# A selective-scan kernel: the gate's second half goes to GpSimd, a row copy goes to VectorE between two halves of a store, and a product is left whole

## The chip, the cores and the metric

The kernel runs on one core of a Trainium2 chip. Its time is device microseconds of that core, as the median of several executions. Tensor work goes to TensorE (PE), and the rest is shared by VectorE (DVE), ScalarE (ACT) and GpSimd (POOL). SyncE (SP) issues most DMAs, GpSimd's queue the others.

## What is computed

Two layers follow each other on an image batch of shape (8, 128, 128, 128). Layer 0 is linear attention with a layer norm and a residual. Layer 1 is a two-dimensional selective scan. The change is in the second part of layer 1, which in the reference reads (cut):

```python
delta = softplus(dt_weight @ dt + bias);  du = delta * u
x_t = exp(delta_t * A) * x_(t-1) + du_t * B_t          # the scan along L, four directions
y   = sum over the four directions of C_t * x_t + D * u
yz  = y * silu(z)                                      # the gate
mu  = yz.mean(-1);  var = ((yz - mu)**2).mean(-1)
out = (gamma * (yz - mu) / sqrt(var + 1e-5) + beta) @ Wout
```

## The kernel before

`layer0` and `layer1_front` write the scan's inputs to DRAM: `ubs` (u times B, in two orders), `xps` (the small rows for delta and C), `zs` (the finished silu(z)) and `gs` (a summand of y). `layer1_scan` reads them. It goes through 8 outer rounds `o`, each of 4 scan slots of 16 chunks, so 512 steps; a chunk is 1024 positions for two halves `c` of 128 channels. All four slots of a round add into one SBUF accumulator `y`.

A step `n` works as follows (line numbers are those of the profile of before):

- `delta` (L973, PE) multiplies into a PSUM tile `px`; `soften` (L977, ACT) makes `sp` by softplus; `decay` (L981, ACT) turns `px` into the factor exp(A times delta); `weigh` (L994, L996, POOL) makes `h`, the product of `ubt` and `sp`; `scan` (L1004, L1006, DVE) runs the recurrence on `px` and `h`, once for each c.
- `spread` (L1012, PE) spreads the C rows over partitions and `emit` (L1024 and others, DVE) multiplies them onto `h`, in two halves; `gather` (L1046, DVE) and `add` (L1054, POOL) add to `y` in the slots after the first.

In the 16 steps after a round's four slots, the chunks of that finished round leave. These are the steps called leaving; they coincide with the first slot of the next round, and after the last round they run without scans. For a leaving chunk, in order: `fetch` loads two tiles `z` (L1070, SP), `gate` multiplies `y` onto `z`, one call for each half (L1074), `square` (L1077, ACT) writes the squares over `y`, `moments` (L1087, PE) makes the rows `pm` of means, `keep` copies `pm` from PSUM to SBUF as `sr` (L1093), `to_tokens` (L1099, PE) turns it into `pq`, `square_mean` (L1103, ACT) makes `mv`, `variance` (L1107, L1108, DVE) makes the variance, `deviation` (L1112, L1113, ACT) its inverse root `rstd`, `project` (L1120, PE) multiplies `z` by the output weights into a `px` tile, and `store` (L1126, DVE, four instructions for each half; L1130 the DMA) scales and writes out. The second half of this chain is one step later than the first: `store` and `deviation` of a chunk run in the step after its `project`.

Every engine's instructions are issued in the order written in `step`. `px` has three buffers, `h` two, `z` six and `r` two. `project` writes into the `px` tile that `scan(n, 1)` has finished with, and that tile is held until the next step's `store` has read it; the second `delta` of the next chunk is written there. In ten or so steps around each leaving group GpSimd's queue also issues `add_d` (L946), an accumulating DMA of 1 MB onto `y`.

Of the kernel before, what the change touches and what calls it, by code (L numbers as in the profile page):

```python
# [11 lines left out]
ALU = mybir.AluOpType  # L12
# [19 lines left out]
CW = CH // H  # L32
# [756 lines left out]
def layer1_scan(ctx: ExitStack, tc, ubs, xps, zs, gs, dtw, dtb, a_log, gamma, beta, w_out, out):  # L789
# [15 lines left out]
    nc = tc.nc  # L805
# [36 lines left out]
    for i in range(3):  # L842
        t = const.tile([P, CH], BF16, name=f"rows{i}")
# [3 lines left out]
    for i in range(3):  # L847
        t = const.tile([P, D2], BF16, name=f"dtw{i}")
# [92 lines left out]
    ubt, sp, da, hs, leaving = {}, {}, {}, {}, {}  # L941
# [6 lines left out]
    def load_rows(n):  # L948
        sl, i = units[n]
        m = sl.at(i)  # L950
        rw = rws[n % 3]
        md = NCH - 1 - m if sl.dt_turned_back else m
        src = xps[sl.dt_image, sl.dt_order].rearrange("j r l -> (j r) l")
        for j in range(3):
            nc.sync.dma_start(rw[3 * NR * j : 3 * NR * j + 3 * NR, :], src[:, md * CH : md * CH + CH])
        nc.sync.dma_start(rw[96:99, :], xps[sl.b, sl.order, :, R + 1, m * CH : m * CH + CH])

    def load(n, c):
        sl, i = units[n]
        m = sl.at(i)  # L960
        ubt[n, c] = wp.tile([P, CH], F32, name="ubt", tag="ub", bufs=4)
        nc.sync.dma_start(ubt[n, c], ubs[sl.b, sl.order, c][:, m * CH : m * CH + CH])
# [16 lines left out]
    def decay(n, c):  # L979
        sl, i = units[n]  # L980
        nc.scalar.activation(da[n, c], sp[n, c], AF.Exp, scale=sa[:, sl.s, c : c + 1])  # L981

    def weigh(n, c):
        if c == 0:
            hs[n] = wp.tile([P, NC2, CH], F32, name="h", bufs=2)
        u, t, h = ubt.pop((n, c)), sp.pop((n, c)), hs[n][:, c, :]
        if units[n][0].permuted:
            u = u.rearrange("p (e h w) -> p h e w", e=2, w=W // 2)
            t, h = (v.rearrange("p (h e w) -> p h e w", e=2, w=W // 2) for v in (t, h))
        else:  # L990
            u, t, h = (v.rearrange("p (h w) -> p h w", w=W) for v in (u, t, h))
        if n in leaving and c == 0:
            for s in (slice(0, CW // 2), slice(CW // 2, CW)):
                nc.gpsimd.tensor_tensor(h[:, s], u[:, s], t[:, s], ALU.mult)  # L994
        else:
            nc.gpsimd.tensor_tensor(h, u, t, ALU.mult)  # L996

    def scan(n, c):
        sl, i = units[n]
# [14 lines left out]
    def emit(n, hf):  # L1014

        sl, i = units[n]
        h = hs[n][:, :, hf * 512 : hf * 512 + 512]
        c = cps.pop((n, hf)).to_broadcast([P, NC2, GN])  # L1020
        if sl.place == 0:
            v = sl.y_at(i, hf)
            split = "p c (a b) -> p c a b"
            nc.vector.tensor_tensor(v, h.rearrange(split, b=H), c.rearrange(split, b=H), ALU.mult)  # L1024
            return
        if hf != sl.first:
            nc.vector.tensor_tensor(h, h, c, ALU.mult)  # L1027
            return
        p = da.pop((n, 1))
        if sl.y_turned:  # L1030
            ts[n] = p.rearrange("p (c b a) -> p c b a", c=NC2, a=GW)
            t = p.rearrange("p (c b a) -> p c a b", c=NC2, a=GW)
            split = "p c (a b) -> p c a b"
            nc.vector.tensor_tensor(t, h.rearrange(split, b=H), c.rearrange(split, b=H), ALU.mult)
        else:
            t = p.rearrange("p (c q) -> p c q", c=NC2)
            ts[n] = t.rearrange("p c (a b) -> p c a b", b=H)
            nc.vector.tensor_tensor(t, h, c, ALU.mult)  # L1038

    def gather(n):  # L1040

        sl, i = units[n]
        v = sl.y_at(i, sl.first)
        if sl.y_turned:
            v = v.rearrange("p c a b -> p c b a")
        nc.vector.tensor_tensor(v, v, ts.pop(n), ALU.add)  # L1046
# [12 lines left out]
    def piece(m, hf):  # L1059
        return y[:, :, (2 * m + hf) * GN : (2 * m + hf + 1) * GN]  # L1060

    def mirrored(o, m, hf):
        p = 2 * m + hf
        return 2 * NCH - 1 - p if o % 2 == 1 else p

    def fetch(o, m):
        for hf in range(2):
            zt[m, hf] = z = wp.tile([P, NC2, GN], F32, name="z", bufs=6)
            p = mirrored(o, m, hf)
            nc.sync.dma_start(z, zs[o].rearrange("c p l -> p c l")[:, :, p * GN : p * GN + GN])  # L1070

    def gate(o, m, hf, eng):
        z, ym = zt[m, hf], piece(m, hf)
        eng.tensor_tensor(z, ym[:, :, ::-1] if o % 2 == 1 else ym, z, ALU.mult)  # L1074

    def square(m, hf):
        nc.scalar.activation(piece(m, hf), zt[m, hf], AF.Square)  # L1077
# [12 lines left out]
    def keep(m):  # L1090
        pm = pts[m, "rows"]
        pts[m, "rows"] = sr = wp.tile([P, GN], F32, name="sr", bufs=1)
        nc.scalar.copy(sr, pm)  # L1093

    def to_tokens(m):
        sr = pts.pop((m, "rows"))
# [13 lines left out]
    def deviation(m):  # L1110
        rstd = rst[m]
        nc.scalar.activation(rstd, rstd, AF.Ln)  # L1112
        nc.scalar.activation(rstd, rstd, AF.Exp, scale=-0.5)  # L1113
# [8 lines left out]
    def store(o, m, hf):  # L1122
        po, rstd = pts.pop((m, hf)), rst[m]
        r = wp.tile([P, GW, P], F32, name="r", bufs=2)
        for w in range(GW):
            nc.vector.scalar_tensor_tensor(r[:, w, :], po[:, w, :], rstd[:, w, hf : hf + 1], bw, ALU.mult, ALU.add)  # L1126
        s = slice(mirrored(o, m, hf) * GW, mirrored(o, m, hf) * GW + GW)

        dst = out[o].rearrange("a e c -> e a c") if o % 4 < 2 else out[o]
        nc.sync.dma_start(dst[:, s, :], r)  # L1130
# [6 lines left out]
    for o in range(B):  # L1137
        n = (o + 1) * K * NCH
# [14 lines left out]
    def step(n):  # L1153
        live = 0 <= n < N
        then = n + 1 < N
        before = 1 <= n <= N
        now, last, soon, later = (leaving.get(n + i) for i in (0, -1, 1, 2))
        first = before and units[n - 1][0].place == 0
        if before:
            half1 = units[n - 1][0].first  # L1160
            emit(n - 1, half1)
            if not first:
                gather(n - 1)
        if now and last:
            gate(*now, 1, nc.vector)
        if before:
            emit(n - 1, 1 - half1)
        if n + 2 < N:
            load_rows(n + 2)
        if n in fetched:  # L1170
            fetch(*fetched[n])
        if last:
            nc.scalar.preload_act_table_set("natural_log_exp_and_others")
        if live:
            decay(n, 0)
        if now:
            square(now[1], 1)
        if live:
            decay(n, 1)
        if last:  # L1180
            deviation(last[1])
        if live:
            weigh(n, 0)
            if n + 2 < N:
                load(n + 2, 0)
        if live:
            weigh(n, 1)
            if n + 2 < N:
                load(n + 2, 1)
        if now:  # L1190
            moments(now[1])
        if live:
            scan(n, 0)
            da.pop((n, 0))
        if last:
            for hf in range(2):
                store(*last, hf)
        if then:
            for c in range(NC2):
                delta(n + 1, c)  # L1200
        if now:
            keep(now[1])
        if then:
            soften(n + 1, 0)
        if now:
            to_tokens(now[1])
            square_mean(now[1])
        if then:
            soften(n + 1, 1)
        if live:  # L1210
            scan(n, 1)
        if first:
            hs.pop(n - 1)
        if now:
            variance(now[1])
        if live:
            half1 = units[n][0].first
            spread(n, half1, "pc")
            spread(n, 1 - half1, "pt")
        if soon and now:  # L1220
            gate(*soon, 0, nc.gpsimd)
        elif soon:
            gate(*soon, 1, nc.gpsimd)
        elif later:
            gate(*later, 0, nc.gpsimd)
        if soon:
            square(soon[1], 0)
        if now:
            p = da.pop((n, 1)) if live else px.tile([P, CH], F32, name="px")
            for hf in range(2):  # L1230
                project(now[1], hf, p[:, hf * 512 : hf * 512 + 512])
        elif live and units[n][0].place == 0:
            da.pop((n, 1))
        if before and not first:
            add(n - 1)
            hs.pop(n - 1)
        if n in weighed:
            units[weighed[n]][0].weights()
        if n in summed:
            add_d(*summed[n])  # L1240
# [78 lines left out]
```

## Time and profile before

| | us |
|---|---|
| Three runs | 9049.44, 9056.5, 9060.8 (median 9056.5) |
| The profiled execution's own time | 9056.52 |
| Its span, first to last instruction | 9054.7 |

| Engine | busy us (share of the span) |
|---|---|
| PE | 6274.4 (69%) |
| DVE | 8055.0 (89%) |
| ACT | 7094.7 (78%) |
| POOL | 7222.8 (80%) |

The mean granted TensorE clock is 0.799. The scans begin near 4350 us and end near 8915 us. A step outside the leaving groups takes 8.22 us. The eight leaving groups begin near 4863, 5445, 6023, 6605, 7183, 7766, 8347 and 8915 us; the seven with scans last 176 to 182 us each, the last one without scans 140 us. Times inside the span are counted from its start. In a line of the timeline, the first two numbers are the start and the length; in brackets is the idle time of the engine before it and what ended that.

### The profile page before, as it was taken

How to read it: one execution, taken by the hardware profiler on the slowest of the kernel's cores; microseconds unless marked ns; L12 is line 12 of the kernel's file. 1: busy time of each engine (PE TensorE's matmuls, PEld its weight loads, DVE VectorE, ACT ScalarE, POOL GpSimd, SP SyncE). 2: the span in 40 equal slices, each digit the busy share in tenths (PEclk: the TensorE clock that was granted, in tenths of full speed). 3: DMA queues.
4: the chain of work that ended last, by engine and by line, in shares of the span. 5: the costliest groups of instructions: out<-in, count | busy, mean ns of one | idle time of the engine just before them, and what ended most of it. 6: DMA issues, size and time to landing. Idle time of an engine off the chain costs nothing. (4 is left out here: it accounts for less than half of the span.)

```text
span 9054.7 us, 91854 instructions
## 1 busy us (share of the span) xinstructions
PE 6274.4 (69%) x24350; PEld 3062.4 (34%) x24512; DVE 8055.0 (89%) x8337; ACT 7094.7 (78%) x8318; POOL 7222.8 (80%) x4676
## 2 busy tenths in 40 slices
PE   8999999998999999997335437355363453644636
PEld 5656655564333333332003204022040230411303
DVE  6777777777999999998899999999999999999996
ACT  5666666665999999997787888878888888888886
POOL 3656765646789888888698897988979989899796
PEclk9999999999999999999556658566585575755857
DMA  1332323423687888888559678596785876958767
GB/s 78 136 119 112 129 101 149 163 91 140 216 245 251 250 244 244 243 245 251 168 170 254 179 211 243 166 244 192 200 255 154 243 205 188 260 155 226 227 177 211
DMA packets 934775, 1750.71 MB, mean 193 GB/s; under 512 B 150228, under 2 KB 376148, under 8 KB 926064
## 3 DMA queue, kind: packets, MB, share of 16 engines
q1 hardware_dynamic: 873328, 1509.92, 50.6%
q0 software_dynamic: 60928, 234.90, 14.1%
q8 instruction: 200, 3.28, 0.1%
q14 instruction: 319, 2.61, 0.1%
HBM read 1052.36 MB, written 692.12 MB: 193 GB/s over the span
## 5 line engine op out<-in xcount | busy, mean ns | idle before, releaser
L973 PE MATMUL px<-rows,dtw 128*128 128x512 bf16 x1893 | 913.5, 575 | 2291.7 <-DVE y L1046 1079.4
L996 POOL TENSOR_TENSOR h<-ubt,sp 128x1024 f32<-128x1024 f32 x912 | 2173.0, 2413 | 244.6 <-DMA rows<-xps 82.7
L575 DVE SCALAR_TENSOR_TENSOR acc<-xb,cw,acc 128x1024 f32<-128x1024 f32 x1024 | 1320.3, 1289 | 132.9 <-ACT xb L543 89.9
L567 POOL TENSOR_TENSOR tap<-tap 128x1024 f32<-128x1024 f32 x512 | 1223.2, 2392 | 249.1 <-ACT tap L565 225.3
L977 ACT ACTIVATE sp<-px 128x1024 f32<-128x1024 f32 x1024 | 1045.9, 1024 | 434.2 <-PE px L973 383.9
L973 PEld LDWEIGHTS <-dtw 128*128 128x128 bf16 x2048 | 166.0, 110 | 3084.3 <-issue 1016.0
L1006 DVE TENSOR_TENSOR_SCAN h<-px,h 128x1024 f32<-128x1024 f32 x512 | 1178.1, 2332 | 34.4 <-POOL h L996 19.0
L1004 DVE TENSOR_TENSOR_SCAN h<-px,h 128x1024 f32<-128x1024 f32 x512 | 1178.8, 2332 | 24.7 <-POOL h L994 9.5
L1054 POOL TENSOR_TENSOR y<-y,h 128x512 f32<-128x512 f32 x768 | 1162.9, 1561 | 4.0 <-DVE h L1027 4.0
L981 ACT ACTIVATE px<-sp,sa 128x1024 f32<-128x1024 f32 x1024 | 1110.2, 1109 | 6.1
L556 PE MATMUL acc<-xi,wt 128*128 128x512 f32 x2048 | 937.6, 600 | 55.0 <-ACT ures L580 55.0
L565 ACT ACTIVATE tap<-xb,cw 128x1024 f32<-128x1024 f32 x768 | 837.3, 1139 | 14.6 <-POOL xb L540 14.5
L977 ACT ACT_TABLE_LOAD x512 | 656.9, 1283 | 159.3 <-PE px L973 125.5
L994 POOL TENSOR_TENSOR h<-ubt,sp 128x512 f32<-128x512 f32 x224 | 368.0, 1692 | 281.6 <-ACT mv L1103 202.2
L1120 PEld LDWEIGHTS px<-wg,z 128*128 128x128 f32 x4096 | 551.1, 217 | 113.0 <-issue 107.9
L1012 PE MATMUL pc<-rows,csel 128*128 128x512 bf16 x1017 | 514.2, 587 | 83.0 <-DVE rstd L1107 73.9
L556 PEld LDWEIGHTS acc<-xi,wt 128*128 128x128 f32 x2048 | 374.8, 189 | 575.1 <-issue 412.5
L1120 PE MATMUL px<-wg,z 128*128 128x128 f32 x4096 | 551.3, 300 | 0.0
L286 POOL TENSOR_TENSOR q<-q,qs 128x512 f32<-128x512 f32 x256 | 270.3, 1056 | 314.1 <-DVE qs L285 250.0
L981 ACT ACT_TABLE_LOAD x400 | 513.2, 1283 | 7.1
L529 PE MATMUL pxb<-xi,wi 128*128 128x512 f32 x1024 | 496.4, 607 | 3.4 <-ACT xb L538 2.0
L1046 DVE TENSOR_TENSOR y<-y,px 128x1024 f32<-128x1024 f32 x384 | 468.6, 1220 | 14.4
(156 smaller groups left out, 15263.1 us busy)
## 6 DMA issues: line engine op xcount, KB each, us to landing
ubt<-ubs SPq DMA_DIRECT2D x1024, 512.0 KB
zs<-z SPq DMA_DIRECT2D x512, 256.0 KB
ubs<-ures SPq DMA_DIRECT2D x256, 512.0 KB
ubs<-turned SPq DMA_DIRECT2D x256, 512.0 KB
z<-zs SPq DMA_DIRECT2D x256, 512.0 KB
y<-gs POOLq DMA_DIRECT2D x128, 1024.0 KB, 10.1
gs<-du POOLq DMA_DIRECT2D x96, 1024.0 KB, 8.6
rows<-xps SPq DMA_DIRECT2D x1536, 60.0 KB
```

What stands on the lines that cost most here:

```text
L556: nc.tensor.matmul(acc[:, s, :], wt[:, j, c, :], x, start=(j == 0), stop=(j == len(ON_PE) - 1))
L565: nc.scalar.activation(t, at(n, c, *d), AF.Copy, scale=weight(n, c, *d))
L567: nc.gpsimd.tensor_tensor(sums[n, c], sums[n, c], t, ALU.add)
L575: nc.vector.scalar_tensor_tensor(acc, at(n, c, *d), weight(n, c, *d), acc, ALU.mult, ALU.add)
L973: nc.tensor.matmul(p[:, hf * 512 : hf * 512 + 512], sl.dw[:, c * P : c * P + P], src, start=True, stop=True)
L977: nc.scalar.activation(t, da[n, c], AF.Softplus)
L981: nc.scalar.activation(da[n, c], sp[n, c], AF.Exp, scale=sa[:, sl.s, c : c + 1])
L996: nc.gpsimd.tensor_tensor(h, u, t, ALU.mult)
L1004: nc.vector.tensor_tensor_scan(e[:, ::-1], x[:, ::-1], e[:, ::-1], start, ALU.mult, ALU.add)
L1006: nc.vector.tensor_tensor_scan(e, x, e, start, ALU.mult, ALU.add)
L1054: nc.gpsimd.tensor_tensor(v[:, c], v[:, c], h[:, c], ALU.add)
L1120: nc.tensor.matmul(po[:, w, :], z[:, c, w * H : w * H + H], wg[:, c, :], start=(c == 0), stop=(c == NC2 - 1))
```

## The change

Three edits, all in the leaving steps. First, both halves of the gate are made by GpSimd, at the end of the step before the one that uses them; before, GpSimd made the first half there, and VectorE made the second at the beginning of the using step, between the two `emit`s. Second, `keep` becomes a VectorE copy, and its place is between the two halves of `store`; before, it was a ScalarE copy ahead of `soften`. Third, GpSimd's product in `weigh` for c = 0, which the leaving steps made in two halves of 128x512, is one instruction of 128x1024.

```diff
@@ weigh
-        if n in leaving and c == 0:
-            for s in (slice(0, CW // 2), slice(CW // 2, CW)):
-                nc.gpsimd.tensor_tensor(h[:, s], u[:, s], t[:, s], ALU.mult)
-        else:
-            nc.gpsimd.tensor_tensor(h, u, t, ALU.mult)
+        nc.gpsimd.tensor_tensor(h, u, t, ALU.mult)
@@ keep
-        nc.scalar.copy(sr, pm)
+        nc.vector.tensor_copy(sr, pm)
@@ step
-        if now and last:
-            gate(*now, 1, nc.vector)
@@ step
         if last:
-            for hf in range(2):
-                store(*last, hf)
+            store(*last, 0)
+        if now:
+            keep(now[1])
+        if last:
+            store(*last, 1)
         if then:
             for c in range(NC2):
                 delta(n + 1, c)
-        if now:
-            keep(now[1])
@@ step
         if soon and now:
-            gate(*soon, 0, nc.gpsimd)
+            for hf in range(2):
+                gate(*soon, hf, nc.gpsimd)
         elif soon:
             gate(*soon, 1, nc.gpsimd)
```

## The prediction

> **What bounds the kernel now.** The page's first part comes first. It says that VectorE is the fullest engine, but as an average over stages.
>
> ```profile
> PE 6274.4 (69%) x24350; PEld 3062.4 (34%) x24512; DVE 8055.0 (89%) x8337; ACT 7094.7 (78%) x8318; POOL 7222.8 (80%) x4676
> ```
>
> The change touches only the leaving steps, so I went to the table of stretches for one group (the one that begins at 6023 us): its steps 1 to 7, and then 8 to 14.
>
> ```profile
> 6033.45:6121.05 87.60, 66.56 (x420) 48.22 (x426) 75.39 (x105) 66.66 (x84) 62.72 (x33) 0.84 0.92 273
> 6121.05:6194.70 73.65, 60.19 (x437) 41.74 (x443) 72.18 (x106) 67.10 (x85) 56.21 (x29) 0.98 0.83 254
> ```
>
> The columns are length, busy PE, PEld, DVE, ACT, POOL, granted clock, DMA share, GB/s. In steps 8 to 14 VectorE is busy 72.2 of 73.65 us: 10.5 us a step, nothing free. Steps 1 to 7 are 14 us longer with a DMA share of 0.92; the list of waits says why (`store` waits for its output buffer):
>
> ```profile
> PE px L973 <- DVE r L1126: 186.0, 110, 6.0
> DVE r L1126 <- DMA out<-r: 65.4, 26, 6.0
> POOL z L1074 <- DMA z<-zs: 44.6, 10, 9.1
> ```
>
> A full VectorE suggests that VectorE sets the step. The timeline of one steady step (12th of the group) asks for more care:
>
> ```profile
> 6173.73 2.35 DVE L1004 TENSOR_TENSOR_SCAN h<-px,h 128x1024 f32<-128x1024 f32 x1
> ...
> 6176.02 2.16 DVE L1126 SCALAR_TENSOR_TENSOR r<-px,rstd,bw 128x128 f32<-128x128 f32 x8
> ...
> 6176.60 0.58 ACT L1093 COPY sr<-pm 128x512 f32<-128x512 f32 x1 [0.61 <-PE pm L1087]
> ...
> 6178.23 0.59 PE L973 MATMUL px<-rows,dtw 128*128 128x512 bf16 x2 [1.34 <-DVE r L1126]
> ...
> 6178.66 0.95 PE L1099 MATMUL pq<-sel,sr 128*128 128x4 f32 x8
> ...
> 6179.65 0.18 ACT L1103 ACTIVATE mv<-pq 128x8 f32<-128x8 f32 x1
> 6179.72 1.02 ACT L977 ACTIVATE sp<-px 128x1024 f32<-128x1024 f32 x1
> ...
> 6180.63 1.06 ACT L1077 ACTIVATE y<-z 128x1024 f32<-128x1024 f32 x1
> ...
> 6181.70 1.28 ACT L1173 ACT_TABLE_LOAD   x1
> ...
> 6183.00 1.12 ACT L981 ACTIVATE px<-sp,sa 128x1024 f32<-128x1024 f32 x1
> ...
> 6184.22 2.35 DVE L1004 TENSOR_TENSOR_SCAN h<-px,h 128x1024 f32<-128x1024 f32 x1
> ```
>
> Read it as one chain with no gap: scan 0 starts at 6173.73, the store ends at 6178.18, and only then may the second `delta` be written (its tile held the projection that the store reads); `pq` stands behind that `delta` on PE, `mv` behind `pq`, the second softplus behind `mv`, then a square, the table load, the decay, which ends at 6184.12, and the next scan 0. That is 10.49 us, and every link starts within 0.1 us of the one before. VectorE's own instructions, start to start, make 10.35 us. So two rings are nearly tied, and the one through PE and ScalarE is ahead by 0.14. The last step of the group decides between them: it has neither the gate nor the square.
>
> ```profile
> 6201.58 2.34 DVE L1024 TENSOR_TENSOR y<-h,pc 128x1024 f32<-128x1024 f32 x2
> 6204.25 2.29 DVE L1004 TENSOR_TENSOR_SCAN h<-px,h 128x1024 f32<-128x1024 f32 x1 [0.33 <-ACT px L981]
> ```
>
> Without the gate (1.22 us) VectorE stands idle for 0.33 us waiting for the decay; the step is 9.54 us, shorter by 0.95. That is the square's place on ScalarE (from the second softplus to the table load it is 1.98 us above, and 1.03 in step 15), not the gate's on VectorE.
>
> **Edit 1, the gate.** 120 VectorE gates of 1.22 us (146 us) go; GpSimd gains 120 of 2.36 us (its own gates' median; 283 us). On VectorE that shortens the ring that is second, so it gives nothing by itself. On GpSimd a steady step now has 2.33 + 2.34 (weigh) + 2 x 2.35 (gates), 9.4 us, against the 8.2 of before. Its first product must wait for scan 1 of the step before (6180.44 in the step above; it starts at 6180.57), because `h` has two buffers. GpSimd was idle 2.3 us there. With the ring found below (11.09) it would be idle for 11.09 - 9.4 - 0.13 = 1.6 us, so the cover holds; with `add_d` (1.2 us) behind the gates it still holds, by 0.4. It doesn't hold in step 0, where `add` is queued behind the gates and the next products behind `add`. There GpSimd has no gap (6024.15 gate, 6026.47 add, 6029.92 product to 6033.42, scan at 6033.45): a second gate adds 2.3, the undivided product takes off 1.1, so +1.2 us once a group. The earlier gate also needs its `z` earlier; where GpSimd already waits for the first `z` (10 times, none in a steady step) the second follows it.
>
> **Edit 2, the copy.** ScalarE loses 128 copies of 0.585 us (75 us). They stand ahead of the table load and the first softplus; the softplus was done at 6179.52 and `mv` started at 6179.65, behind `pq`. ScalarE had time there, so nothing comes back. VectorE gains 128 copies of 128x512 out of PSUM. The trace has no such copy; two rows bound it: 0.29 us (128x128 out of PSUM, L879) and 0.68 us (128x512 with one PSUM operand, L300). I take 0.68, because 129 columns out of PSUM (L253, 0.283) cost what one column a cycle and a fixed part cost. Consecutive instructions overlap by 0.08 (eight of 0.342 in 2.16 us), so 0.60 in the queue.
>
> Behind the copy stand the second half of the store, scan 1, the variance and the emits. Waiting for the store are the second `delta`, `pq`, `mv`, the second softplus, the square, the table, the decay and scan 0: the leading ring. Before, the copy was beside it. Now the ring is 10.49 + 0.60 = 11.09 us. `pm` is ready at 6176.57; the copy's turn would come at 6173.73 + 2.29 + 1.04 = 6177.06, so it doesn't usually wait; where the clock is low `pm` is up to 1.2 us later, and then the store waits too.
>
> The page "VectorE: DVE Perf Modes" of the Trainium skill (section "The perf-mode tier table") allows a copy out of PSUM up to twice the rate. By its cycle table that is (120 + 256) / 0.96, an estimate of 0.39 us, 0.31 in the queue, and the sum below would be 28 us instead of 49. No run here shows a double rate out of PSUM.
>
> **Edit 3, the product.** 112 products of 1.28 + 2.28 us (the second stretched by 1.0 beside VectorE's gate) become 2.38. GpSimd's saving of 1.1 us a step shortens the wait ahead of scan 0, which is now not the last to arrive: nothing, except in step 0, counted above.
>
> **The sum.** A group with scans:
> - step 0: +1.2;
> - steps 1 to 7: 7 x 0.60 = +4.2. They take 86.5, 83.0, 87.6, 82.8, 88.6, 84.4 and 84.3 us in the seven groups against 73.4 for seven steady ones, so 12 us a group are DMA backlog. A slower pace lets the backlog shrink. If the transfers set the time, the 5.4 of steps 0 to 7 are hidden; if not, none. The share of 0.92 is near full: I count a third, 1.8;
> - steps 8 to 15: 8 x 0.60 = +4.8.
>
> That makes 6.6 a group, 46 for seven. The last group has no scans; there PE's chain moments, copy, `pq`, project (7.3 us a step) holds the copy, 0.68 for 0.585: 16 x 0.1 = 1.6, and perhaps as much for `z` waited for earlier: 3. In all +49. The profiled execution (9056.52, span 9054.7) is the median of the runs, so 9106.
>
> Ends: everything hidden in steps 0 to 7, 34 + 2, is 9092; nothing hidden, 7 x 10.2 + 3, is 9131; with a late `pm` in some steps up to 9150; with the short copy (0.29, 0.21 in the queue) and all hidden, about 9070.
>
> **Rivals.**
> - *VectorE is the ring.* Then 1.13 goes and 0.60 comes, -0.53 in 105 steps, -56, with step 0's +8: 9008. It decides if the decay isn't what scan 0 waits for. For it: 72.2 busy of 73.65. Against it: the idle 0.33 in step 15. Chance 0.09.
> - *All is hidden*: the transfers set more steps than I think, or the copy is short. 9056 to 9074. Chance 0.08.
> - *The port.* L1108, 8 columns, takes 0.17 us in most steps and up to 2.38 where a GpSimd instruction runs; it is issued at 6180.53, 0.04 ahead of GpSimd's product. If it now falls behind an undivided product, it waits 2.4 and the emits with it: the step becomes 6.71 + 0.60 + 2.5 + 2.5 = 12.3, 1.8 more than now in 105 steps, 9245. Both start from scan 1's end as before, so the order should stand. Chance 0.05.
>
> The page "SBUF — State Buffer" (section "Who interferes with whom") gives the rule: the port that VectorE shares with GpSimd is locked for a whole instruction. L1108's rows agree, and by the rule leaving the product whole doubles the longest block.
>
> **How the numbers follow.** The forecast has 0.78, up to 9150. A measurement of this kernel tells 0.2%, 18 us, from no change. Faster 0.09, same 0.08, slower 0.83. The range 9064 to 9150 leaves out the first rival, the third, and the edges of the others.
>
> **What would show it.** Right: steady steps near 11.1 us, scan 0 idle before on ScalarE's L981 by about 0.9, the copy at 0.68 directly ahead of the second four stores, step 0 near 11.8, GpSimd idle some 1.6 a step. Wrong: steady steps at 10 us (first rival), L1108 over 2 us in steady steps (third), or a copy near 0.4.

## The result, and the profile after

The changed kernel takes **9131.1 us** (median of 5 runs, 9119.2 to 9137.9) against 9056.5 (9049.4 to 9060.8): a ratio of 1.0079, 95% interval [1.0065, 1.0093], slower by 74.6 us. Its profiled execution took 9129.67 (span 9127.9), 73.15 more than the one of before, and all sums below are made against that difference.

The page's first part:

```profile
PE 6321.5 (69%) x24512; PEld 3073.3 (34%) x24512; DVE 8042.8 (88%) x8345; ACT 7023.1 (77%) x8190; POOL 7378.0 (81%) x4684
```

VectorE's and ScalarE's shares fell, GpSimd's rose, and the span grew by 73 us. The table of stretches for the group that now begins at 6041.69 (step 0, steps 1 to 7, steps 8 to 14; columns as before):

```profile
6041.69:6053.50 11.81, 7.98 (x57) 5.28 (x50) 11.60 (x7) 8.96 (x11) 11.73 (x7) 0.93 0.84 230
6053.50:6137.65 84.15, 66.06 (x433) 46.55 (x434) 70.61 (x105) 61.26 (x74) 71.07 (x33) 0.86 0.93 277
6137.65:6216.30 78.65, 63.03 (x437) 43.96 (x435) 68.72 (x106) 63.49 (x78) 65.35 (x29) 0.93 0.78 238
```

Steps 8 to 14: 78.65 us where they took 73.65, with VectorE *less* busy (68.7 for 72.2). In step 0 GpSimd has no gap. One steady step in the timeline (the 11th of that group), from scan 0 to scan 0:

```profile
6171.40 2.35 DVE L1000 TENSOR_TENSOR_SCAN h<-px,h 128x1024 f32<-128x1024 f32 x1 [1.26 <-ACT px L981]
...
6173.69 1.13 DVE L1122 SCALAR_TENSOR_TENSOR r<-px,rstd,bw 128x128 f32<-128x128 f32 x4
...
6174.74 0.68 DVE L1089 COPY sr<-pm 128x512 f32<-128x512 f32 x1
...
6175.34 1.11 DVE L1122 SCALAR_TENSOR_TENSOR r<-px,rstd,bw 128x128 f32<-128x128 f32 x4
...
6176.50 0.59 PE L973 MATMUL px<-rows,dtw 128*128 128x512 bf16 x2 [1.72 <-DVE r L1122]
...
6177.92 0.18 ACT L1099 ACTIVATE mv<-pq 128x8 f32<-128x8 f32 x1 [0.74 <-PE pq L1095]
...
6182.49 2.35 DVE L1000 TENSOR_TENSOR_SCAN h<-px,h 128x1024 f32<-128x1024 f32 x1 [1.27 <-ACT px L981]
```

The step is 11.09 us. The copy stands between the store's halves, the second `delta` (L973) waits for the second half, `mv` for the `pq` behind it, and scan 0 waits 1.27 us for the decay.

By stretches, summed over the seven groups with scans (after less before):

| stretch | measured | forecast |
|---|---|---|
| step 0 | +8.3 | } 12.6 for steps 0 to 7 |
| steps 1 to 7 | +10.6 | } |
| steps 8 to 14 | +34.9 | 29.4 |
| step 15 | +2.3 | 4.2 |
| last group, without scans | +14.2 | 3 |
| before the first scan, untouched | +4.0 | 0 |
| other steps, untouched | -1.2 | 0 |
| all | +73.15 | +49 |

### The profile page after: what moved, and what is told of

Same layout as the page of the kernel before. It is cut to its first block, busy times and chain, and to the rows that moved or that the text cites. A ratio compares the mean times of both kernels' runs of the same rounds, so it can differ in the third digit from the quotient of the medians.

```text
span 9127.9 us, 92102 instructions
## 1 busy us (share of the span) xinstructions
PE 6321.5 (69%) x24512; PEld 3073.3 (34%) x24512; DVE 8042.8 (88%) x8345; ACT 7023.1 (77%) x8190; POOL 7378.0 (81%) x4684
## 5 line engine op out<-in xcount | busy, mean ns | idle before, releaser
L992 POOL TENSOR_TENSOR h<-ubt,sp 128x1024 f32<-128x1024 f32 x1024 | 2410.0, 2393 | 458.6 <-ACT mv L1099 161.8
L973 PE MATMUL px<-rows,dtw 128*128 128x512 bf16 x2048 | 954.9, 565 | 2280.5 <-DVE y L1042 1058.6
L973 PEld LDWEIGHTS <-dtw 128*128 128x128 bf16 x2048 | 165.5, 110 | 3111.1 <-issue 1045.3
L1070 POOL TENSOR_TENSOR z<-y,z 128x1024 f32<-128x1024 f32 x256 | 615.2, 2472 | 48.0 <-DMA z<-zs 45.8
```

Source lines behind the costliest of these rows:

```text
L973: nc.tensor.matmul(p[:, hf * 512 : hf * 512 + 512], sl.dw[:, c * P : c * P + P], src, start=True, stop=True)
```

## The experiments

Each ratio compares with runs of the kernel before that were taken along with the experiment (medians 9050.9 to 9058.2 us). Steps and stretches are read from one profiled execution of each kernel and compared with the profile of before; single executions of one kernel lie up to 33 us apart, so a few us in one stretch mean little.

Two new things in the trace of after had to be placed. The copy comes late in some steps (15 of 49 steady steps are over 11.4 us), and one small VectorE instruction, the variance's `tensor_scalar` (L1104, 128x8, 0.17 us alone), can take far longer. All its executions, and one in the timeline beside GpSimd:

```profile
L1104 DVE TENSOR_SCALAR rstd<-rstd x128: 170/171/11657, 4872.4 to 9118.9; 128x8 f32<-128x8 f32 x128
```

```profile
5472.26 5.12 POOL L992 TENSOR_TENSOR h<-ubt,sp 128x1024 f32<-128x1024 f32 x2
...
5472.64 9.61 DVE L1104 TENSOR_SCALAR rstd<-rstd 128x8 f32<-128x8 f32 x1
5476.91 5.08 POOL L1070 TENSOR_TENSOR z<-y,z 128x1024 f32<-128x1024 f32 x2
```

Durations are least/median/most in ns. In step 1 of five groups it stays open through four GpSimd instructions that follow each other without a gap; in the last group's first step it takes 11.66 us. In three of the five groups the two emits and the next scan, which read one operand from PSUM, start meanwhile, and they are open until the same moment as the small instruction, 0.25 us after the last of the four; whether they too wait for GpSimd isn't shown:

```profile
6646.07 1.19 POOL L946 DMA_DIRECT2D y<-gs  x1
...
6646.56 10.27 DVE L1104 TENSOR_SCALAR rstd<-rstd 128x8 f32<-128x8 f32 x1
...
6646.64 10.20 DVE L1020 TENSOR_TENSOR y<-h,pc 128x1024 f32<-128x1024 f32 x2
...
6650.25 6.58 DVE L1002 TENSOR_TENSOR_SCAN h<-px,h 128x1024 f32<-128x1024 f32 x1
```

"Excess" below is the time of all 128 beyond 0.17 each: 39 us before (most: 2.38), 100 after.

### Each half of the change alone

**copy_only**: the kernel before with edit 2.

```
-        nc.scalar.copy(sr, pm)
+        nc.vector.tensor_copy(sr, pm)
...
-            for hf in range(2):
-                store(*last, hf)
+            store(*last, 0)
+        if now:
+            keep(now[1])
+        if last:
+            store(*last, 1)
```

> The kernel before with edit 2 alone: the copy on VectorE between the halves of the store; VectorE keeps its gate and the product stays divided. If scan 0 is set by the ring store, second delta, pq, mv, second softplus, square, table, decay (A), a steady leaving step is 10.49 + 0.60 = 11.09 us with scan 0 waiting about 0.1 us for the decay, as in the changed kernel, step 0 stays at 10.62, and no variance instruction waits more than 2.4 us. With half of the 4.2 us of steps 1 to 7 hidden by the transfers and 4.8 in steps 8 to 15, 7 x 6.9 + 2 = +50: 9106 us. If VectorE's queue sets it (B), a steady step is 10.35 + 0.60 = 10.95 with no wait for the decay, some 9090 us.

Measured 9108.3, ratio 1.0064 [1.0051, 1.0076]. The steady step is 11.08, step 0 10.62 as before, steps 8 to 14 +34.6, the last group +10.0, steps 1 to 7 only +3.7; the excess is 19 us.

**gate_only**: edits 1 and 3; the copy stays on ScalarE, at its old place.

```
-        if now and last:
-            gate(*now, 1, nc.vector)
...
-            gate(*soon, 0, nc.gpsimd)
+            for hf in range(2):
+                gate(*soon, hf, nc.gpsimd)
```

> The changed kernel without edit 2: the copy is on ScalarE again, at its old place; both gates on GpSimd, product whole. A: VectorE is relieved of 1.13 us a step but a steady step stays at 10.49 us, with scan 0 waiting about 1 us for the decay; step 0 is 11.8 (GpSimd), and the variance instruction of step 1 and of the last group's first step is caught behind GpSimd for 8 to 12 us as in the changed kernel, part of it hidden by the transfers: +8 for step 0, +14 in the last group, 0 to 20 in steps 1 to 7: 9078 to 9098 us. B: steady steps under 10 us and a time under 9010.

Measured 9070.3, ratio 1.0020 [1.0011, 1.0029]. A steady step:

```profile
6161.74 2.35 DVE L1000 TENSOR_TENSOR_SCAN h<-px,h 128x1024 f32<-128x1024 f32 x1 [1.26 <-ACT px L981]
...
6172.23 2.35 DVE L1000 TENSOR_TENSOR_SCAN h<-px,h 128x1024 f32<-128x1024 f32 x1 [1.26 <-ACT px L981]
```

It is 10.49 us, as before: VectorE lost its gate and spends the time waiting for the decay. Step 0 is 11.81 (+8.3 in all), and the excess is 128 us, so the long waits come with edits 1 and 3. They cost next to nothing here: summed over the seven groups, steps 1 and 2 are 35 us longer than before, but steps 3 to 7, where the kernel before has its backlog of transfers, are 35 us shorter, and the last group is only 2.5 longer. The halves, +57.4 and +19.4 by their own comparisons, make 76.8 against 74.6 for the whole.

### What the small instruction's wait costs

**var_psum**: the changed kernel, with the variance's difference left in PSUM, so that L1104's successor (L1105) reads PSUM.

```
+        v = pts.pop(m)[:, :, :, 1]
+        nc.vector.tensor_tensor(v, v, mv.pop(m), ALU.subtract)
+        nc.vector.tensor_scalar(rstd, v, 0.0, EPS1, ALU.max, ALU.add)
```

> The changed kernel with the variance's difference left in PSUM, so that the second of its two small VectorE instructions reads PSUM and writes SBUF instead of SBUF to SBUF. If that instruction's long waits (3.7 to 4.2 us in step 0, 9.6 to 10.3 in step 1 of five groups, 11.7 in the last group) are for the port that VectorE shares with GpSimd, they are gone and it takes under 0.3 us everywhere; the last group loses about 10 us, steps 1 to 7 a few us a group at most because the transfers hide a part: 9095 to 9121 us. If it waits for something else, a result of GpSimd for one, the long waits stay, and the time is that of the changed kernel within 8 us. Steady steps stay at 11.08 or rise by the second spread, which now waits for one more small instruction.

Measured 9150.7, ratio 1.0110 [1.0096, 1.0123]. No execution is long any more:

```profile
L1105 DVE TENSOR_SCALAR rstd<-pq x128: 166/167/168, 4868.3 to 9127.3; 128x8 f32<-128x8 f32 x128
```

But the time was missed by 30 us, to the wrong side. Steps 8 to 14 are +48.4, many at 11.7 to 12.9, and steps 1 to 7 are +12.2 although no execution waits. The second `spread` writes the PSUM bank that `pq` sits in and now waits for one instruction more (TensorE idle 0.92 us ahead of it, for 0.70); the projections and `pm` follow it. That this is the whole cause isn't shown.

**first_gate**: the changed kernel, with the second gate of each group's second chunk on VectorE again.

```
+        if now and last and n - 2 not in leaving:
+            gate(*now, 1, nc.vector)
...
-            for hf in range(2):
+            for hf in range(2 if last else 1):
```

> The changed kernel, but the second gate of a group's second chunk is made by VectorE between the emits as before; all other gates stay on GpSimd. If step 0 costs +1.2 because of that gate in GpSimd's queue, step 0 is back at 10.6 or below (the product is whole, so down to 10.0). If the variance instruction's long waits need a GpSimd queue that never pauses, they shrink to under 4.5 us in step 1 and in the last group, because GpSimd has its gap again. Then -8 to -12 for step 0, some -10 in the last group and a few in steps 1 to 7: 9095 to 9112 us. If the accumulating DMAs of GpSimd's queue cause the waits, they stay at 9 to 12 us.

Measured 9109.4, ratio 1.0064 [1.0051, 1.0076]. The longest L1104 is 3.1 us and the excess 35; steps 1 to 7 are 14 us better than in the changed kernel, the last group 6. The run doesn't separate the two causes that its forecast names, the missing pause and the accumulating DMA: here L1104 never starts while GpSimd's queue is at `add_d`. Step 0 was a miss: 11.6 us, not 10.6. VectorE's gate there takes 2.43 us instead of 1.22, beside the undivided product:

```profile
6048.53 5.67 POOL L992 TENSOR_TENSOR h<-ubt,sp 128x1024 f32<-128x1024 f32 x2
6049.53 2.43 DVE L1070 TENSOR_TENSOR z<-y,z 128x1024 f32<-128x1024 f32 x1
```

**var_stt**: the changed kernel, with the `tensor_scalar` exchanged for a `scalar_tensor_tensor` (the constant in a tile).

```
-        nc.vector.tensor_scalar(rstd, rstd, 0.0, EPS1, ALU.max, ALU.add)
+        nc.vector.scalar_tensor_tensor(rstd, rstd, 0.0, eps1, ALU.max, ALU.add)
```

> The changed kernel with one instruction exchanged: the variance's tensor_scalar (clamp, add a constant) becomes a scalar_tensor_tensor of the same place, shape and result, with the constant in a 128x8 tile. In first_gate and var_psum the long waits of that instruction went away, but each time with something else moved. Theory A (the wait is a matter of the form tensor_scalar with both operands in SBUF, and it costs time): no such instruction over 0.4 us, where the changed kernel has 29 that together take 99.7 us longer than 0.17 us each; the time falls by what first_gate gained in steps 1 to 7 and in the tail, 13.8 + 5.7 us at most, 9109 to 9124 us. Theory B (the wait is hidden): the waits go and the time stays, 9125 to 9137. If the waits stay, the cause is not the form.

Measured 9128.1, ratio 1.0080 [1.0067, 1.0092], where the changed kernel has 1.0079. The new instruction waits like its predecessor, up to 11.39 us (excess 76). So the form is not the cause; what var_psum took away was an operand in SBUF.

### The ring's other links

**copy_behind**: the changed kernel, copy behind both halves of the store (`store` 0, `store` 1, `keep`).

> The changed kernel with the copy behind both halves of the store instead of between them, still on VectorE. If the whole cost of edit 2 is its place in the ring (A), the second delta is written at 4.50 us after scan 0's start again instead of 5.11, and only pq still waits for the copy (done near 5.05): mv near 6.3 instead of 6.51, a steady step of 10.9 us instead of 11.08. If an added VectorE instruction costs its length wherever it stands (B), a steady step stays at 11.08. Time under A 9110 to 9120, under B 9131.

Measured 9140.4, ratio 1.0089 [1.0076, 1.0103]: a miss. The steady step did shorten, to 10.76 in most cases (steps 8 to 14 +25.1), but steps 1 to 7 are +22.3 and the last group +23.0; the excess is 126, with six waits over 10 us.

**soft_first**: the changed kernel, both softplus ahead of `mv` in ScalarE's order.

```
             soften(n + 1, 0)
+            soften(n + 1, 1)
...
-        if then:
-            soften(n + 1, 1)
```

> The changed kernel with one more exchange and no work less: ScalarE makes both softplus ahead of the small square of the means (mv), so that the second softplus waits for the second delta and no longer for pq. A: the second softplus starts at about 5.75 us after scan 0 instead of 6.6, and the ring store, delta, softplus, (mv), square, table, decay takes about 10.4 us a steady step instead of 11.08: -0.7 in 105 steps, 9060 to 9080 us. If the softplus waits for something else, or VectorE's queue sets the step (B), steady steps stay at 11.08 and the time at 9131.

Measured 9121.8, ratio 1.0069 [1.0056, 1.0082]: a miss in the time, though the steady step is 10.35, as theory A had it (steps 8 to 14 only +5.2). `mv` had cost the ring 0.7 us. It is given back in steps 1 to 7, +41.8: the excess is 131, and a wait of 10.22 us there delays step 2 to 19.8.

**soft_behind**: both of these.

> The changed kernel with both exchanges: the copy behind the whole store, and both softplus ahead of mv. A: the second delta at 4.5, the second softplus at 5.5, mv at 6.4 behind pq, the decay's end near 9.9: a steady step of about 10.0 us, 0.5 under the kernel before, with VectorE's own queue (9.83) just behind. Step 0 stays 11.8, the variance instruction's long waits in step 1 and in the last group stay. -1.1 in 105 steps against the changed kernel, part of it hidden by the transfers in steps 1 to 7: 9025 to 9050 us, so at or under the kernel before. B: no change from soft_first.

Measured 9186.1, ratio 1.0142 [1.0127, 1.0158], the largest miss. 82 of 128 executions are over 0.3 us (excess 207), and 32 of these sit in steps 8 to 14, where the changed kernel has none. One of them:

```profile
6172.43 4.68 POOL L992 TENSOR_TENSOR h<-ubt,sp 128x1024 f32<-128x1024 f32 x2 [1.46 <-DMA z<-zs]
...
6173.20 1.62 DVE L1104 TENSOR_SCALAR rstd<-rstd 128x8 f32<-128x8 f32 x1
```

**before_soft**: the kernel *before* with both softplus ahead of `mv`.

> The kernel before with that one exchange alone: both softplus ahead of mv. A: the ring through ScalarE falls from 10.49 to about 10.26 us, so that VectorE's own queue (10.35) is the longer: steady steps of 10.35 to 10.40, -0.1 in 105 steps, 9035 to 9047 us. If the ring through ScalarE was not what set the step, no change.

Measured 9059.8, ratio 1.0008 [1.0000, 1.0017]: theory A's gain didn't come (steps 8 to 14 are only -2.4, with five over 11.4 us where before has two). The steady step is 10.35 us with VectorE idle for 0.3 us in four steps together: the second ring of the prediction, at the length it was given there.

### Does the pace bring the wait?

**quick**: gate_only, with both softplus ahead of `mv` and var_stt's instruction. **quick_first**: the same, with step 0 as before (gate on VectorE, the product beside it divided).

> Edits 1 and 3 without the copy's move (the copy stays on ScalarE, as in gate_only), both softplus ahead of mv (as in soft_first), and the scalar_tensor_tensor of var_stt. Theory A (ring): soft_first's steady step is 10.35 us with the copy's 0.60 in it; without it the ring is 9.75, VectorE's queue 9.2, GpSimd 9.4, ScalarE 9.7 with the copy, so the steady step is 9.8 to 10.1. Against gate_only (9070) that is 0.4 to 0.7 us in each of 49 steps 8 to 14, 20 to 34 us, and steps 0 to 7 change little: 9036 to 9052. Rival (at this pace GpSimd, TensorE at its lower clock or the loads end the step): the steady step stays at 10.3 or above, 9060 to 9072.

> quick, with step 0 of each group as in the kernel before: the second gate of the second chunk on VectorE, and the product that runs beside it divided in two halves. Theory (step 0's loss of 1.2 us is GpSimd's fourth gate, and first_gate kept it because VectorE's gate waited 2.43 us beside the undivided product): step 0 is 10.6 again, 8 us below quick: 9028 to 9044. Rival (step 0 is set elsewhere in this order): step 0 stays at 11.6 to 11.8 and the time is quick's.

Measured 9127.2, ratio 1.0082 [1.0069, 1.0096], and 9123.1, ratio 1.0082 [1.0068, 1.0095]: both 75 to 95 us above what the ring promised. quick_first has step 0 back at 10.62, and steps of 9.84 occur in both, but between them stand steps of 11.3 to 12.9. One of these in quick:

```profile
6165.04 0.17 DVE L1105 TENSOR_TENSOR rstd<-pq,mv 128x8 f32<-128x8 f32 x1
6165.24 2.35 DVE L1106 SCALAR_TENSOR_TENSOR rstd<-rstd,eps 128x8 f32<-128x8 f32 x1
6167.52 2.34 DVE L1022 TENSOR_TENSOR y<-h,pc 128x1024 f32<-128x1024 f32 x2
```

```profile
6165.22 4.68 POOL L994 TENSOR_TENSOR h<-ubt,sp 128x1024 f32<-128x1024 f32 x2 [2.00 <-ACT mv L1101]
```

The product starts 0.02 us ahead of the small instruction, which then ends with the first of the two; the emits stand behind it. 90 and 83 of 128 executions are over 0.3 us.

**quick_relu**: quick_first without that instruction. The clamp is a Relu on ScalarE, the constant the logarithm's bias.

```
-        nc.vector.scalar_tensor_tensor(rstd, rstd, 0.0, eps1, ALU.max, ALU.add)
...
-        nc.scalar.activation(rstd, rstd, AF.Ln)
+        nc.scalar.activation(rstd, rstd, AF.Relu)
+        nc.scalar.activation(rstd, rstd, AF.Ln, bias=eps1)
```

> quick_first without the variance's second instruction on VectorE: its clamp at zero is a Relu on ScalarE ahead of the logarithm (0.2 us more there), its constant is the logarithm's bias. In quick and quick_first a steady step is 9.84 us where that small instruction takes 0.17 us, and 11.3 to 12.9 where it starts just behind GpSimd's product and takes 1.23 to 2.35 (90 and 83 of 128 are over 0.3 us). Theory A (that wait, and not TensorE, the loads or ScalarE, is what those orders lost): most steady steps are 9.8 to 10.1, 0.4 to 0.7 below before in 49 steps, 20 to 34 us, with steps 0 as before and steps 1 to 7 within 10 us of before: 9022 to 9045, ahead of the kernel before. Rival (the moments or the loads come late at this pace in any case): steps of 11 to 13 us stay among those of 9.84 and the time is 9055 to 9110.

Measured 9055.9 (11 runs) beside 9058.2 for before (15 runs), ratio 0.9999 [0.9990, 1.0008]. Taking the instruction away is worth 67 us against quick_first (9123.1), 72 with each one's own runs of before, so the wait is what the quick orders lost. The absolute forecast was missed by 11 us: a steady step is 10.25, not 9.84, and some reach 12.8. In the former the `store` now waits 0.27 us for the inverse root, which has one instruction more on ScalarE; the rest of the 0.41 isn't placed. For the latter see the projection, at two clocks:

```profile
6120.15 6.21 PE L1122 MATMUL px<-wg,z 128*128 128x128 f32 x32
...
6144.16 3.73 PE L1122 MATMUL px<-wg,z 128*128 128x128 f32 x32
```

In the step after the first of these `pm` is late, and ScalarE waits 2.82 us for it. No version here beats the kernel before.

## Why the prediction was right, and where it was off

The ring that leads, the copy's length and its full price in a steady step were right. The end, 74.6 us where 49 were forecast, lies in the range's upper half. That it equals the 9131 given for "nothing hidden" is luck: half of that term was hidden, and late `pm`, the last group and 4 us ahead of the first scan made up for it.

- **The leading ring** (10.49, through the store, second `delta`, `pq`, `mv`, second softplus, decay) stood. gate_only takes 1.13 us a step from VectorE and the step stays at 10.49; before_soft shortens the ring and stops at VectorE's own 10.35. Both lengths are those that were read from the trace of before. That scan 0 waits 1.27 us for the decay, and not the "about 0.9" under the signs, follows from the prediction's own terms: 11.09 less VectorE's 10.35 - 1.13 + 0.60.
- **Edit 2.** The copy takes 0.68 us, as its nearest row said:

```profile
L1089 DVE COPY sr<-pm x128: 662/681/692, 4869.4 to 9116.7; 128x512 f32<-128x512 f32 x128
```

The estimate of 0.39 us took the double rate from the table of the Trainium skill's page "VectorE: DVE Perf Modes" (section "The perf-mode tier table"). That was a misreading: further down, the same section limits a PSUM operand to the single rate for fp32, and the 0.68 us measured here for 512 fp32 columns agrees. The steady step became 11.09, as worked out.
- **Late `pm`.** It was named for the upper end and left out of the sum; in steps 8 to 14 it is the missing term. The copy waited in 43 leaving steps (list of waits). 14 of them are steady ones, all with a step over 11.4 us, and together wait 5.3 us; one of the 14:

```profile
DVE sr L1089 <- PE pm L1083: 28.7, 43, 3.5
```

```profile
6186.31 0.69 DVE L1089 COPY sr<-pm 128x512 f32<-128x512 f32 x1 [0.41 <-PE pm L1083]
```

49 steps at a median of 11.08 in place of 10.49 give +29; the steps above the median add 8.0 us after and 2.3 before. Together 35, as measured. The granted clock in those steps was 0.98 before (mean over the groups) and 0.93 after, and copy_only has the same 0.93: 6 stretches at half the clock lay in them before, 22 do after, and ahead of each of the 14 late copies there is one. Why they come back isn't shown; the step's length alone doesn't decide, since copy_behind, with 10.76, has 32.
- **Step 0.** +1.2 a group forecast, +1.19 measured, GpSimd without a gap. The variance's wait there (3.7 to 4.2 us) isn't the cause: var_psum, where nothing waits, has the same 11.82.
- **Steps 0 to 7: the mis-sized share.** The prediction let a third of 5.4 us a group count. 2.7 came, half. copy_only shows what was right: its copies alone add 3.7 us in all seven groups' steps 1 to 7 (7 x 4.2 = 29 if nothing were hidden), so backlog does hide them. The other 7 come when the long waits of L1104 are added, and first_gate, which takes these away, is 14 us better there. But gate_only has the waits at no cost in these steps, and var_psum has +12.2 without them: that waits and longer steps together are more than the backlog can hide would fit all of these but var_psum, and isn't shown.
- **The last group: the term mis-sized most.** A settled step there did grow as forecast, from 7.29 to 7.40 us. But its first steps lost another 12. copy_only (+10.0) has projections of 6.38, 5.77 and 5.17 us there, where the others, and all 16 of before, take 3.82, and a store that waits 8.06 us for its output buffer:

```profile
8971.51 6.38 PE L1120 MATMUL px<-wg,z 128*128 128x128 f32 x32
```

```profile
9000.00 1.13 DVE L1126 SCALAR_TENSOR_TENSOR r<-px,rstd,bw 128x128 f32<-128x128 f32 x4 [8.06 <-DMA out<-r]
```

The changed kernel has three such projections (6.30, 5.95, 5.21) and the wait of 11.66, after which its first store comes 8.4 us later than before's. What that wait adds isn't shown: gate_only and var_stt have the same late first store and end at +2.5 and +7.4.
- **The port** was given 0.05, for steady steps, and there it didn't happen: L1104 takes 0.17 us and starts 0.04 ahead of the product. It came where GpSimd's queue had been made gapless, in steps 0 and 1 and the last group, which the prediction didn't ask about. Nor did it double the longest wait, as the prediction has it from the undivided product: the most was 2.38 us before and is 11.66 after. quick shows the rival as described, as soon as steps are near 9.8 us.
- **+4.0 before the first scan** is not the change's: over the variants this untouched part differs from before by -0.6 to +6.2.

## What to carry to other kernels

When two rings are nearly tied, cost each edit on both, and read from an odd step (here the last of a group) which one leads: work put on a leading ring is paid in every step, work taken off the other gives nothing. Before filling an engine's gaps, ask which small instruction of another engine used them; here a 0.17 us instruction paid up to 11.7. A shorter ring helps only if its orders still start in the same sequence: look at margins of 0.02 to 0.04 us as carefully as at the length.

## What the runs showed of the hardware

The Trainium skill's page "SBUF — State Buffer" (section "Who interferes with whom") lets a VectorE instruction contend with GpSimd when it has two inputs in SBUF, or one and a two-port mode, and blocks the later one for the whole instruction. The runs agree on who waits: the `tensor_scalar` on SBUF (up to 11.66 us, and 11.87 in gate_only) and the `scalar_tensor_tensor` on SBUF (up to 11.58), not the same `tensor_scalar` reading PSUM (166 to 168 ns), nor the subtraction with one operand in PSUM (0.14 to 0.17 us beside the same products). They differ on how long: it is not one instruction but, in some steps, four, where GpSimd issues them back to back. In others it gets in between the first two. Twelve of the runs, with before and after, have this instruction on SBUF, and 50 of its executions take over 8 us: 43 of these start while GpSimd's queue is at `add_d` (L946 in the lines above) and 6 while it is at `add`. (`add_d` is issued in 16 steps for each leaving group, not in ten or so; four of them are its steps 1, 2, 3 and 5.) Beside a product alone it got in within 2.4 us in 332 of 333 executions. But five that start beside `add_d` in var_stt, with the same four instructions to come, took 0.17 us, and no run moves `add_d` alone, so what decides isn't shown.

The page "TensorE: Matmul & The Clock Gate" (Part 1, "The HAM clock gate") says that the array runs at a half or the full clock, chosen by windows of about 3.4 us. The clock records agree (stretches of 3.413 us at 0.5), and the same projection takes 3.73 us or up to 6.38. Here a step longer by 0.59 us, with the same matmuls, came with more such stretches and cost 35 us in 49 steps instead of 29.
